# Layer 0 of a two-layer macaron model: query-state products on GpSimd, a fourth output chunk sorted by expert, and scratch rows cleared by nine writes

## The chip, the cores and the metric

The kernel runs on one core of a Trainium2 chip. The metric is the device time of one execution in microseconds (us), lower is better. The core has five engines with a queue of instructions each: TensorE (PE), VectorE (DVE), ScalarE (ACT), GpSimd (POOL) and SyncE (SP). Each engine takes its queue strictly in order, so an instruction that waits holds up everything behind it. DMA transfers are started from the queues of SP, ACT and POOL. A difference of about 0.5% (4.6 us) is what a measurement of this kernel can tell from no change.

## The reference

There are 8 sequences of 256 tokens with 128 features. Two layers follow each other, and each is feed-forward, attention, feed-forward, all with residuals. In layer 0 the feed-forward part sends each token to its two best of 8 experts (hidden width 512), and the attention is a delta-rule recurrence over time, for 16 heads of width 8:

```
def step(M, inp):
    q_t, k_t, v_t, b_t = inp
    out_t = einsum('bnh,bnhd->bnd', q_t, M)          # the query-state product
    retrieved = einsum('bnhd,bnd->bnh', M, k_t)
    delta = v_t - retrieved
    M = M + b_t[..., None, None] * einsum('bnh,bnd->bnhd', k_t, delta)
    return M, out_t
```

Step t needs the state that step t-1 left, so the 256 steps can't run side by side. Batch and head together (8 x 16) fill the 128 partitions. Layer 1 has ReLU attention, and experts (hidden width 256) that each choose their 256 best tokens.

## The kernel before

**Tiles and chunks.** A tile is 16 time steps of all 8 sequences, 128 tokens; there are 16 tiles (0 to 15). `CHUNKS` (line 30) groups them as 3, 4, 4, 3 and 2 tiles. Layer 0 is a pipeline over these chunks. "In" calls are the first feed-forward part (in 0, in 1 and in 2, where in 2 covers the last three chunks together). Then `prepare` (line 850) makes keys, values and queries of a chunk, `steps` (line 982) runs its part of the recurrence, `finish` (line 1050) turns states into attention output, and "out" calls (out 0 to out 4, one for each chunk) are the second feed-forward part.

**The recurrence** is on DVE: six small instructions a step (lines 1024 to 1038 and 1007), 16 steps a tile. When a tile's states are complete, `finish` multiplies them with the queries: one DVE instruction of 128 x 1024 a tile, `qm` (line 1064), with the normalised queries `qn` made once a chunk (line 972). PE adds up the products (`pm`, line 1070), ACT copies them, and two DMAs, a square, a mean, a root and a matmul follow until `x` is updated (line 1112).

**An expert call** comes in two forms. A *dense* call (`dense`, line 617) sends the chunk's tokens through all 8 experts: 32 matmuls of 128 x (128 n) for n tiles (line 639) and 32 n of 128 x 128 (line 649). A *sorted* call (`gates` 321, `route` 420, `scattering` 494, `fetching` 678, `experts` 697, `combining` 784) computes the two experts of each token, writes the tokens to DRAM rows ordered by expert with indirect DMAs on POOL's queue (line 503, two for each tile), reads them back (line 689), and runs one expert for each row tile: four 128 x 128 matmuls in (line 764) and four out (line 743). The results go to DRAM (line 727) and come back by indirect DMAs on POOL's queue (line 834), and matmuls add them up (lines 809 and 812). Each row tile loads its own expert's weights of 514 KB (line 568). Before, in 1, in 2, out 0, out 1 and out 2 are sorted; in 0, out 3 and out 4 are dense (line 226). The unfilled DRAM rows must be zero: `clearing` (line 519) writes 37 blocks of 128 x 256 numbers from the tile `zero`.

**The order of the work** is fixed when the program is built. A planner, `Weave` (line 42), runs generators; each yields an engine and an estimated time, and the planner gives the next place to the one that could start first, and among equals to the one of higher rank. The estimates only set the order on each queue: at run time semaphores decide. A yield on "pool" also charges DVE 0.5 us in the plan (line 100). Streams wait for marks such as ("states", t), ("x", key) or ("free", tag, number); `acquire` (line 600) hands out buffers. The gates of out c wait for `finish(c)` and for the result of out c-2 (line 1122), and PE takes the calls in the order in 0 to out 4 (line 1125). Layer 1 starts when PE is through with out 4 (line 1421) and when `moving` (line 1143) has carried the tokens into layer 1's layout: half 0 after chunk 2, half 1 after out 4 (line 1163).

Of the kernel before, what the change touches and what calls it, by code (L numbers as in the profile page):

```python
# [17 lines left out]
P = 128  # L18
# [9 lines left out]
F0, F1 = 512, 256  # L28

CHUNKS = [(0, 3), (3, 4), (7, 4), (11, 3), (14, 2)]  # L30
BANKS = {"h": 3, "y": 2, "m": 2, "f": 1}
CAP = B * S // E

SORTED = NT // 2
# [7 lines left out]
class Weave:  # L42
# [27 lines left out]
    def run(self, streams):  # L70
        for rank, s in streams:
            self.spawn(s, rank)
        streams, at, nexts = self.streams, self.at, self.nexts
        while any(n is not None for n in nexts):
            best = None
            for i, n in enumerate(nexts):
                if n is None:
                    continue
                if n[0] in self.free:
                    start = max(at[i], self.free[n[0]])  # L80
                elif n[0] == "until":
                    start = max(at[i], n[1])
                elif n in self.done:
                    start = max(at[i], self.done[n])
                else:
                    continue
                if best is None or (start, -self.ranks[i], at[i]) < best[:3]:
                    best = start, -self.ranks[i], at[i], i
            if best is None:
                raise RuntimeError([(st.__name__, n) for st, n in zip(streams, nexts) if n])  # L90
            start, _, _, i = best
            self.rank = self.ranks[i]
            if nexts[i][0] in self.free:
                engine, us, lag, table = nexts[i] + (None, None, LAGS[nexts[i][0]], None)[len(nexts[i]) :]
                if table and table != self.table:
                    self.load(table)  # L96
                    self.table = table
                    us += 1.3
                self.free[engine] = start + us
                if engine == "pool":  # L100
                    self.free["dve"] += 0.5
                start += us + lag
            at[i] = self.now = start
            nexts[i] = next(streams[i], None)
# [3 lines left out]
def kernel(ctx: ExitStack, tc: tile.TileContext, a: dict, out: bass.AP):  # L108
# [58 lines left out]

    x1 = const.tile([P, NT, D], F32, name="x1")

    zero = const.tile([P, 2 * D], F32, name="zero")  # L170
    pool.memset(zero, 0.0)
    rows0 = load("rows0", 5 * D + NH + 1, act)
    wqT, wkT, wvT, woT, b2 = (rows0[:, i * D : (i + 1) * D] for i in range(5))
    b2 = b2[:E, :]
# [21 lines left out]
    def woven(dram, moe, pools):  # L196
# [26 lines left out]
        calls["in", 2] = t0, NT - t0  # L223
        for c in range(n_c):
            calls["out", c] = CHUNKS[c]
        is_sorted = set(calls) - {("in", 0), ("out", n_c - 2), ("out", n_c - 1)}
        unsorted = [key for key in calls if key not in is_sorted]
        chosen = {}

# [10 lines left out]
        def vec(n):  # L240

            return "dve", 0.07 + 0.00105 * n, 0.14
# [145 lines left out]
        def turned_gates(key, g, m):  # L388

            name = "b" + "".join(map(str, key))  # L390
            gate = chosen[key]["gate"]
            if True:
                b = yield from acquire("m")
                yield "pe", 0.15 * m
                pg = bank("m", b, [E, TB, P], f"pg{name}_{g}")
                for i in range(m):
                    pe.transpose(pg[:, i, :], gate[:, g + i, :], ident)
                yield "act", 0.1 + 0.13 * m
                gT = work.tile([E, BW], F32, name=f"gT{name}_{g}", tag="gT", bufs=1)
                act.copy(gT[:, : m * P], pg[:, :m].rearrange("p a b -> p (a b)"))  # L400
                mark(("free", "m", b))
            return gT

        def biasing(key):

            t0, m = calls[key]
            gT = yield from turned_gates(key, 0, m)
            b = yield from acquire("m")
            yield "pe", 0.23 * m
            pb = bank("m", b, [P, TB, D], f"pb{key[0]}{key[1]}")  # L410
            for i in range(m):
                pe.matmul(pb[:, i, :], lhsT=gT[:, i * P : (i + 1) * P], rhs=b2, start=True, stop=True)
            xs = x[:, t0 : t0 + m, :]
            yield vec(m * D)
            dve.tensor_tensor(xs, xs, pb[:, :m], ALU.add)
            mark(("free", "m", b))
            mark(("biased", key))
# [91 lines left out]

        def dram_rows(i, nt):  # L510

            wide = -(-nt // 2) * 2
            rows = [
                nc.dram_tensor(f"rows_{i}_{k}", [m * P, D], F32, kind="Internal").ap()
                for k, m in enumerate((wide, nt))
            ]
            return rows

        def clearing():

            for k, ((rows, _), us) in enumerate(zip(buffers, (15.0, 45.0, 300.0, 340.0))):
                yield "until", us
                n = rows.shape[0] // P // 2
                for i in range(n):
                    yield "sp", 0.4, 2.0
                    sync.dma_start(
                        out=rows.rearrange("(r p w) d -> r p (w d)", p=P, w=2)[i], in_=zero
                    )
                mark(("clear", k))

# [253 lines left out]
        def combining(key, parts):  # L784


            t0, n = calls[key]
            name = "c" + "".join(map(str, key))
            yield "computed", key
            c = chosen[key]  # L790
            got = {}

            def joined(what, g, m):
                gT = yield from turned_gates(key, g, m)
                if m > 2:
                    yield "got", key, 2 * (g + m) - 5
                b = yield from acquire("m")
                pb = bank("m", b, [P, TB, D], f"pb{name}_{g}")
                for i in range(m):

                    gates = moe.tile([P, 2, P], F32, name=f"dg{name}_{g}_{i}", tag="dg")
                    for k in range(2):
                        yield "act", 0.28
                        act.activation(
                            gates[:, k, :], half_ident, AF.Copy, scale=c["p"][k][:, g + i : g + i + 1]
                        )
                    yield "got", key, 2 * (g + i) + 1
                    yield "pe", 0.75
                    pe.matmul(pb[:, i, :], lhsT=gT[:, i * P : (i + 1) * P], rhs=b2, start=True, stop=False)
                    for k in range(2):  # L810
                        j = 2 * (g + i) + k
                        pe.matmul(
                            pb[:, i, :], lhsT=gates[:, k, :], rhs=got.pop(j), start=False,
                            stop=k == 1,
                        )
                        mark(("back", key, j))
                xs = x[:, t0 + g : t0 + g + m, :]
# [149 lines left out]
        def queries(c, q, inverse):  # L967
            n = CHUNKS[c][1]
            inv = yield from inverse(2, q)
            qn = scan.tile([P, CT, HD], F32, name=f"qns{c}", tag="qn")[:, : n * SL]  # L970
            yield vec(2 * n * P)
            dve.tensor_tensor(qn, q.rearrange("p h t -> p t h"), bc(inv, HD), ALU.mult)
            prepared[c, "q"] = qn
            mark(("queries", c))

# [74 lines left out]
        def finish(c):  # L1050
# [5 lines left out]
            yield "queries", c  # L1056
            for i in range(n):
                yield "states", t0 + i
                yield "dve", 1.15
                qn = prepared[c, "q"]  # L1060
                M = states.pop(t0 + i)
                ts = slice(i * SL, (i + 1) * SL)
                qm = scan.tile([P, SL, HD, HD], F32, name=f"qm{name}_{i}", tag="qm")
                dve.tensor_tensor(qm, M[:, :, :, :HD], bc(qn[:, ts], HD), ALU.mult)  # L1064
                mark(("summed", t0 + i))
                yield "pe", 1.8

# [763 lines left out]
```

## Time and profile before

| what | value |
|---|---|
| median of 3 runs (lowest to highest) | 921.16 us (921.13 to 925.2) |
| the profiled execution: time, span of its profile | 919.45 us, 917.7 us |
| mean granted clock of PE | 0.884 |
| PE busy | 728.3 us, 79% |
| DVE busy | 537.8 us, 59% |
| ACT busy | 453.9 us, 49% |
| POOL busy | 153.9 us, 17% |
| tile 0 of the recurrence starts, tile 15 ends | 121.1 us, 453.9 us |
| PE on out 2 (sorted), out 3 (dense), out 4 (dense) | 435.6 to 475.2, 475.2 to 528.1, 528.1 to 557.7 us |

The profile gives, for one execution, the busy time of each engine, a picture of the span in 40 slices with a digit for the busy tenths of each slice, the chain of work that ended last, groups of equal instructions with their count, mean duration and the idle time in front of them, and tables of any stretch of time. All times in us count from the start of the span. A line Lnnn is the line of the kernel that issued the instruction.

### The profile page before, as it was taken

What the parts mean: (1) busy time and instruction counts of PE and PEld (TensorE: products, weight loads), DVE (VectorE), ACT (ScalarE), POOL (GpSimd) and SP (SyncE); (2) the same over time, 40 slices, a digit from 0 to 9 for tenths busy, and PEclk for the clock granted to TensorE, in tenths of its full rate; (3) what the DMA queues carried; (4) which work ended last, traced back from release to release, by engine and by line L of the source; (5) the groups of instructions that cost most, each with busy time, mean ns of one, the idle gap of its engine ahead of it and who ended that gap; (6) DMA issues with size and microseconds to landing.
All of it is one profiled execution on the core that took longest, in us unless ns stands there. A gap on an engine that the chain in (4) does not pass through costs nothing.

```text
span 917.7 us, 16688 instructions
## 1 busy us (share of the span) xinstructions
PE 728.3 (79%) x5243; PEld 586.6 (64%) x5243; DVE 537.8 (59%) x3223; ACT 453.9 (49%) x1067; POOL 153.9 (17%) x263
## 2 busy tenths in 40 slices
PE   3999559985399647854999999994889999999671
PEld 2778459884268437843997796763755556666471
DVE  2433176676599899887711422577347766658741
ACT  3556245772178604841674555431456666673231
POOL 0030712005400230033003000003031111100303
PEclk9999779997589657975899999898799999999976
DMA  4367585963557336926583331005210000000352
GB/s 187 104 176 207 151 261 180 268 211 101 187 143 234 80 127 196 244 63 200 160 252 96 113 113 30 0 1 162 89 55 2 2 2 2 2 1 0 119 157 76
DMA packets 101160, 109.07 MB, mean 119 GB/s; under 512 B 38736, under 2 KB 79056, under 8 KB 101072
## 3 DMA queue, kind: packets, MB, share of 16 engines
q1 hardware_dynamic: 96544, 98.42, 35.6%
q0 software_dynamic: 4096, 8.40, 2.9%
q10 hardware_dynamic: 432, 1.20, 0.4%
q8 instruction: 41, 0.67, 0.3%
q14 instruction: 47, 0.39, 0.1%
HBM read 85.11 MB, written 22.87 MB: 118 GB/s over the span
## 4 chain that ended last, share of the span: by engine, by line
PE 36%; DVE 15%; DMA 5%; ACT 4%; issue 4%; SPq 2%; POOL 1%; another core or an unknown queue 0%; POOLq 0%; DVEq 0%; ACTq 0%
PE ps L1636 3%; PE pa L1680 3%; PE phf L1436 3%; PE pydout L649 3%; PE phdout L639 3%; PE pyf L1453 3%; PE phpout L764 2%; DVE x L1483 2%; DVE ge0f L1321 2%; PE pypout L743 2%; PE pypf L743 2%; PE phpf L764 1%; PE pmo L1070 1%; DMA xs<-rows 1%; DVE ge1f L1321 1%
## 5 line engine op out<-in xcount | busy, mean ns | idle before, releaser
L1453 PEld LDWEIGHTS pyf<-w_W,hf 128*128 128x128 f32 x512 | 71.0, 200 | 26.0 <-issue 22.6
L1453 PE MATMUL pyf<-w_W,hf 128*128 128x128 f32 x512 | 76.0, 287 | 2.6 <-DVE x L1483 2.1
L1007 DVE TENSOR_TENSOR mk<-Ms,kns 128x72 f32<-128x72 f32 x251 | 56.3, 224 | 25.4 <-ACT Ms L961 23.7
L1436 PE MATMUL phf<-xTf,w_W 128*128 128x512 f32 x128 | 67.9, 616 | 0.0
L1442 ACT ACTIVATE hf<-phf 128x512 f32<-128x512 f32 x64 | 37.8, 597 | 59.9 <-PE phf L1436 57.6
L1070 PE MATMUL pmo<-qmo,ident 128*128 128x128 f32 x256 | 38.9, 314 | 29.3 <-DVE qmo L1064 19.4
L1034 DVE TENSOR_TENSOR Ms<-Ms,u 128x64 f32<-128x64 f32 x251 | 53.9, 215 | 13.6 <-DVE e L1002 8.3
L768 ACT ACTIVATE hpin<-phpin,w 128x128 f32<-128x128 f32 x160 | 45.7, 379 | 24.7 <-remote 12.3
L743 PE MATMUL pypin<-w,hpin 128*128 128x128 f32 x320 | 46.7, 295 | 13.3 <-ACT hpin L768 8.1
L768 ACT ACTIVATE hpout<-phpout,w 128x128 f32<-128x128 f32 x172 | 49.1, 374 | 16.4 <-PE phpout L764 14.8
L1002 DVE TENSOR_REDUCE e<-mk 128x8 f32<-128x72 f32 x251 | 54.6, 218 | 3.7 <-DVE u L1029 3.3
L1070 PEld LDWEIGHTS pmo<-qmo,ident 128*128 128x128 f32 x256 | 36.3, 226 | 32.0 <-DVE qmo L1064 21.8
L96 ACT ACT_TABLE_LOAD x43 | 55.2, 1283 | 3.0 <-issue 2.2
L1038 DVE SCALAR_TENSOR_TENSOR r<-kbs,dot,e 128x8 f32<-128x8 f32 x251 | 54.9, 219 | 2.8 <-DVE Ms L1034 2.7
L1029 DVE TENSOR_TENSOR u<-kbs,r 128x64 f32<-128x64 f32 x256 | 56.3, 220 | 0.2
L743 PEld LDWEIGHTS pypin<-w,hpin 128*128 128x128 f32 x320 | 43.3, 209 | 14.7 <-ACT hpin L768 8.9
L1652 DVE TENSOR_SCALAR w<-ps 128x512 f32<-128x512 f32 x64 | 42.5, 684 | 16.0 <-PE ps L1636 12.7
L764 PE MATMUL phpout<-xTpout,w 128*128 128x128 f32 x344 | 49.1, 290 | 2.2 <-ACT xTpout L718 2.2
L643 ACT ACTIVATE hdout<-phdout,w 128x384 f32<-128x384 f32 (+1 forms) x64 | 32.3, 526 | 34.0 <-PE phdout L639 26.9
L764 PE MATMUL phpin<-xTpin,w 128*128 128x128 f32 x320 | 47.5, 298 | 0.7 <-issue 0.7
L503 POOL DMA_INDIRECT rows<-xnf,slotrf x16 | 15.8, 985 | 188.7 <-DVE pastrf L479 184.3
L764 PEld LDWEIGHTS phpout<-xTpout,w 128*128 128x128 f32 x344 | 44.9, 205 | 3.4 <-ACT xTpout L718 3.2
(360 smaller groups left out, 1762.1 us busy)
## 6 DMA issues: line engine op xcount, KB each, us to landing
w<-in_w_dram SPq DMA_DIRECT2D x107, 514.0 KB
w<-in_w_dram SPq DMA_DIRECT2D x30, 256.0 KB
xs<-rows SPq DMA_DIRECT2D x24, 256.0 KB
rows<-zero SPq DMA_DIRECT2D x37, 128.0 KB
rows<-ypin SPq DMA_DIRECT2D x9, 256.0 KB
rows<-ypout SPq DMA_DIRECT2D x9, 256.0 KB
w_W<-in_w_dram SPq DMA_DIRECT2D x8, 256.0 KB
dts<-sps SPq DMA_DIRECT2D x6, 256.0 KB
```

The costliest lines, as they stand in the source:

```text
L96: self.load(table)
L743: pe.matmul(py[:, t % TB, :], lhsT=h[:, g, :], rhs=second(w, g), start=g == 0, stop=g == n_f - 1)
L764: pe.matmul(ph[:, f, :], lhsT=first(w, f), rhs=xT[:, t % TB, :], start=True, stop=True)
L768: act.activation(h[:, f, :], ph[:, f, :], AF.Relu, bias=bias(w, f))
L1002: dve.tensor_reduce(e, mk, AX.X, ALU.add)
L1007: dve.tensor_tensor(mk, M(t), bc_mid(kn[:, t + 1], HD), ALU.mult)
L1029: dve.tensor_tensor(u, bc(kb[:, t], HD), bc_mid(r, HD), ALU.mult)
L1034: dve.tensor_tensor(M(t + 1)[:, :, :HD], M(t)[:, :, :HD], u, ALU.add)
L1038: dve.scalar_tensor_tensor(r, kb[:, t], dot, e, ALU.mult, ALU.add)
L1070: pe.matmul(pm, lhsT=ident, rhs=qm[:, :, h, :], start=h == 0, stop=h == HD - 1)
L1436: pe.matmul(ph, lhsT=W[:, e, f * P : (f + 1) * P], rhs=c["xT"][k], start=True, stop=True)
L1453: pe.matmul(py[:, i, :], lhsT=before[0][ff][:, i * P : (i + 1) * P], rhs=second(W[:, before[3]], ff), start=ff == 0, stop=ff == n_f - 1,)
```

## The change

1. The products `qm` (16 of 128 x 1024) and the normalised queries `qn` (5) are issued on GpSimd in place of VectorE. The planner is told 2.4 us for a product and 0.2 + 0.3 n for queries of n tiles, and charges DVE 0.5 us only for GpSimd work under 1.5 us.
2. out 3 becomes a sorted call: 13 row tiles, in place of 8 experts on 3 tiles.
3. The 37 clearing writes become 9, of up to 12 tiles each, from the tile `x1`, which GpSimd sets to zero at the start and which nothing else uses until layer 1. The rows are no longer rounded up to even numbers of tiles.
4. The buffer `gT` of the turned gates gets a lock in the planner (`gates`, one place), freed after the matmuls that read it, and in `joined` the wait for gathered rows comes ahead of the turning of the gates.

```
-BANKS = {"h": 3, "y": 2, "m": 2, "f": 1}
+BANKS = {"h": 3, "y": 2, "m": 2, "f": 1, "gates": 1}
...
-                if engine == "pool":
+                if engine == "pool" and us < 1.5:
                     self.free["dve"] += 0.5
...
-    zero = const.tile([P, 2 * D], F32, name="zero")
-    pool.memset(zero, 0.0)
+    pool.memset(x1[:, : (NT + E) // 2, :], 0.0)
...
-        is_sorted = set(calls) - {("in", 0), ("out", n_c - 2), ("out", n_c - 1)}
+        is_sorted = set(calls) - {("in", 0), ("out", n_c - 1)}
...
-            if True:
-                b = yield from acquire("m")
...
-            return gT
+            room = yield from acquire("gates")
+            b = yield from acquire("m")
...
+            return gT, room
...
-                n = rows.shape[0] // P // 2
-                for i in range(n):
+                n = rows.shape[0] // P
+                for r in range(0, n, (NT + E) // 2):
+                    m = min(n - r, (NT + E) // 2)
                     yield "sp", 0.4, 2.0
                     sync.dma_start(
-                        out=rows.rearrange("(r p w) d -> r p (w d)", p=P, w=2)[i], in_=zero
+                        out=rows[r * P : (r + m) * P].rearrange("(p w) d -> p w d", p=P), in_=x1[:, :m, :]
                     )
...
             def joined(what, g, m):
-                gT = yield from turned_gates(key, g, m)
                 if m > 2:
                     yield "got", key, 2 * (g + m) - 5
+                gT, room = yield from turned_gates(key, g, m)
...
-            yield vec(2 * n * P)
-            dve.tensor_tensor(qn, q.rearrange("p h t -> p t h"), bc(inv, HD), ALU.mult)
+            yield "pool", 0.2 + 0.3 * n
+            pool.tensor_tensor(qn, q.rearrange("p h t -> p t h"), bc(inv, HD), ALU.mult)
...
-                yield "dve", 1.15
+                yield "pool", 2.4
...
-                dve.tensor_tensor(qm, M[:, :, :, :HD], bc(qn[:, ts], HD), ALU.mult)
+                pool.tensor_tensor(qm, M[:, :, :, :HD], bc(qn[:, ts], HD), ALU.mult)
```

Built, the change also alters the queues. On POOL, around the end of the recurrence, the order is now: the gathers of out 1, six of the eight scatters of out 2, the product of tile 14, the last two scatters of out 2, the product of tile 15, the six scatters of out 3. On PE, the sums of tile 14's products and the gates of out 3 come ahead of the experts of out 2, the combine of out 2 stands among the row tiles of out 3, the gates of out 4 behind the last of them, and the combine of out 3 among the dense experts of out 4. On DVE, the first step of chunk 1 now comes behind the update of `x` by `finish(0)`.

More of the change, by code (lines that the diff above doesn't have):

```diff
@@ L391, in turned_gates @@
             gate = chosen[key]["gate"]
-            if True:
-                b = yield from acquire("m")
[L394 to L401, printed above, removed]
-            return gT
+            room = yield from acquire("gates")
+            b = yield from acquire("m")
+            yield "pe", 0.15 * m
+            pg = bank("m", b, [E, TB, P], f"pg{name}_{g}")
+            for i in range(m):
+                pe.transpose(pg[:, i, :], gate[:, g + i, :], ident)
+            yield "act", 0.1 + 0.13 * m
+            gT = work.tile([E, BW], F32, name=f"gT{name}_{g}", tag="gT", bufs=1)
+            act.copy(gT[:, : m * P], pg[:, :m].rearrange("p a b -> p (a b)"))
+            mark(("free", "m", b))
+            return gT, room
         def biasing(key):
             t0, m = calls[key]
-            gT = yield from turned_gates(key, 0, m)
+            gT, room = yield from turned_gates(key, 0, m)
             b = yield from acquire("m")
@@ L412, in biasing @@
                 pe.matmul(pb[:, i, :], lhsT=gT[:, i * P : (i + 1) * P], rhs=b2, start=True, stop=True)
+            mark(("free", "gates", room))
             xs = x[:, t0 : t0 + m, :]
@@ L510, in dram_rows @@
         def dram_rows(i, nt):
-            wide = -(-nt // 2) * 2
             rows = [
-                nc.dram_tensor(f"rows_{i}_{k}", [m * P, D], F32, kind="Internal").ap()
-                for k, m in enumerate((wide, nt))
+                nc.dram_tensor(f"rows_{i}_{k}", [nt * P, D], F32, kind="Internal").ap() for k in range(2)
             ]
@@ L816, in joined @@
                         mark(("back", key, j))
+                mark(("free", "gates", room))
                 xs = x[:, t0 + g : t0 + g + m, :]
```

## The prediction

> **What bounds the kernel now.** I read the picture of the span first: which engine is full where.
>
> ```profile
> PE   3999559985399647854999999994889999999671
> DVE  2433176676599899887711422577347766658741
> POOL 0030712005400230033003000003031111100303
> PEclk9999779997589657975899999898799999999976
> ```
>
> A digit is 22.9 us. In slices 11 to 19 (252 to 459 us) DVE, which runs the recurrence, is at 8 or 9 tenths nearly throughout, and PE falls to 3 twice. From slice 20 to 27 (459 to 642 us) PE is full and DVE falls to 1 to 5. So two bounds follow each other: the recurrence on DVE until 454 us, then PE with out 2, out 3 and out 4. The table of stretches gives the prices: tile 4 (210.7), tile 11 (357.9), out 3 (475.2) and out 4 (528.1).
>
> ```profile
> core 0: us, PE busy (x) PEld busy (x) DVE busy (x) ACT busy (x) POOL busy (x), PEclk, DMA share, GB/s
> 210.70:240.20 29.50, 12.57 (x63) 9.56 (x63) 15.55 (x127) 4.58 (x13) 19.99 (x21) 0.60 0.53 176
> 357.90:369.70 11.80, 11.80 (x108) 11.80 (x107) 11.80 (x109) 7.50 (x25) 0.00 (x0) 1.00 0.84 268
> 475.20:528.10 52.90, 50.41 (x309) 39.97 (x308) 13.56 (x63) 26.53 (x52) 9.06 (x50) 1.00 0.40 124
> 528.10:557.70 29.60, 29.60 (x207) 27.67 (x206) 7.68 (x30) 15.80 (x35) 0.00 (x0) 1.00 0.26 82
> ```
>
> Sixteen bare steps take 11.8 us (tile 11). Tile 4, beside 21 indirect DMAs on POOL, takes 29.5. The chain of waits shows how the two bounds meet: out 2's rows arrive, PE goes through out 2, out 3 and out 4 without a break worth naming, and the second half of layer 1's input is loaded right behind.
>
> ```profile
> 429.38 6.14 DMA xs<-rows
> 435.57 1.13 PE ptpout L714 x4
> ...
> 473.37 1.79 PE pypout L743 x16
> 475.16 3.87 PE phdout L639 x12
> ...
> 555.04 2.69 PE pydout L649 x24
> 561.56 1.53 DMA xd<-x
> 563.31 3.98 DMA x<-xd
> ```
>
> From here every us by which out 4 ends earlier or later is carried to the end: layer 1 keeps its order on PE. So I sum the shift of out 4's end, 557.7.
>
> **Products on GpSimd: the price.** The groups by form:
>
> ```profile
> L1064 DVE TENSOR_TENSOR qmo<-Ms,qns 128x1024 f32<-128x1024 f32 x16 | 19.4, 1214 | 0.0
> L1589 POOL TENSOR_TENSOR xba<-xna,w_rows 128x256 f32<-128x256 f32 x8 | 5.9, 732 | 59.3 <-ACT xna L266 59.3
> ```
>
> On DVE a product delays the next step by 1.14 (the 1.21 of the row overlaps it a little). On POOL a quarter of it takes 0.73; with 0.09 fixed (a one-column memset on POOL takes 89 ns) the whole takes 0.64 x 4 + 0.09 = 2.65 us. `qn` of four tiles: 1.03 on DVE, 0.64 x 2 + 0.09 = 1.37 on POOL.
>
> What a product on POOL costs the recurrence beside it, the trace doesn't show: no GpSimd tensor_tensor runs there, and in layer 1 none lies beside a DVE instruction with two inputs in SBUF. I bound it.
> - At best nothing: DVE gains 1.14 for each tile.
> - The middle row is tile 4. Of its 17.7 us over the bare time, 3.3 are other DVE work and 3.05 one wait for PE; the other 11.3 over 21 indirect DMAs make 0.54 for each 0.95 us of POOL, 57%. For 2.65 that is 1.5, a net loss of 0.4 a tile.
> - At worst DVE stands still for all of the 2.65: a net loss of 1.5. A row shows such a standstill: two equal instructions on DVE, the second beside a memset on POOL.
>
> ```profile
> 472.31 0.23 DVE L1185 TENSOR_SCALAR row_e<-row_e 128x128 int32<-128x128 int32 x1
> 472.49 0.50 DVE L1186 TENSOR_SCALAR row_e<-row_e 128x128 int32<-128x128 int32 x1
> ```
> ```profile
> 472.50 0.42 POOL L1561 MEMSET va<- 128x334 f32 x1
> ```
>
> The second took 0.50 for 0.23 and ended 0.07 behind the memset's end (472.92): it waited the memset out whole. Five of the six instructions of a step read two SBUF tensors, as a product on POOL also does, and this is the row nearest to compute work on both engines. I take the worst end as the likeliest, and keep all three.
>
> [...]
>
> **Shift of the recurrence at the end of tile 14** (435.6 now), the point that matters below. Products of tiles 3 to 13 lie in front of it, 11 of them; those of tiles 0 to 2 only meet DVE's wait for chunk 1 (172.7 to 192.3). Four `qn` lie there too (0.6 to 1.0 on DVE, 0.86 on average; 0.3 dearer on POOL). The first step of chunk 1 now stands behind `finish(0)`, whose update of `x` came at 193.5, behind the start at 190.2: +3. Against that, DVE stood idle for others (PE, ACT, DMA) in waits over 0.3 us for about 15 us between 200 and 436, of which I let half absorb a loss, or half as much (3) eat a gain.
> - Worst: 11 x 1.5 + 1.2 + 3 - 7 = +14.
> - Middle: 11 x 0.4 + 1 + 3 - 2 = +6.
> - Best: -11 x 1.14 - 3.4 + 3 + 3 = -10.
>
> **A wait that the change adds on POOL.** Behind the product of tile 14 stand out 2's last two scatters. Now the scatters run free of it:
>
> ```profile
> 416.40 1.04 POOL L503 DMA_INDIRECT rows<-xngout,slotrout  x1 [7.82 <-issue]
> ...
> 425.36 0.98 POOL L503 DMA_INDIRECT rows<-xngout,slotrout  x1 [0.30 <-issue]
> ```
>
> The last ends at 426.3, and PE gets the rows 9.2 later (landing, SP's read, transposes at 435.57). Behind the product they end at 435.7 + 2.65 + 0.3 + 2.25 = 440.9, and PE starts at 450.1: **+14.6**, plus the shift of tile 14. Who waits: SP's read of the rows, then PE, which has nothing else placed ahead. The gathers of out 1, now behind the product of tile 13 (411.7), come some 16 us later than 398.6; they delay out 3's gates, not yet the path.
>
> **PE on out 2** took 39.6. The sums of tile 14 (2.3), the gate matmuls of out 3 (1.2) and the bias of dense out 3 (1.4) leave this stretch, out 3's routing matmuls (2) come in: **-2.6**.
>
> **out 3 sorted, and out 4.** A row tile is eight 128 x 128 matmuls, 0.89 for four (rows L764 and L743, two records a matmul): 1.78. Thirteen: 23.1; transposes 2; out 2's combine in between 3.5; filling the pipeline 2: 30.6. Then out 4's gates: from the update of `x` by out 2 to the router matmuls 6.8 passed, of which 2.4 lie beside the last row tile: 4.4. Dense out 4: 29.6 as now, plus out 3's combine 2.8, plus gates, bias and heads that stood in out 3 (2.6), plus 3 for gathers that PE meets early: the first combine of out 2 came 13.4 behind its last expert, PE now asks after 11. That is 38. In all 73, against 82.5 now (475.2 to 557.7): **-9.5**. The saving on matmuls alone is larger: dense out 3 is 32 x 0.645 + 96 x 0.2225 = 42, sorted 23.1. The rest is spent on the way to DRAM and back. Five more weight loads of 514 KB hide: 13 in 30 us is 226 GB/s, and tile 11's stretch moved 268. If they don't, each costs 1.9. out 3's scatters come behind the product of tile 15: 454 + 14 + 2.65 + 0.3 + 7.6 + 9.2 = 488, and out 2's experts hold PE until 501, so they are covered.
>
> **Clearing and locks** I cost at nothing. The nine writes fall between 5 and 62 us and near 300 and 340; PE has one idle stretch over 1 us between its first matmul at 13.35 and 100 us, and weights are held five ahead. If a write of 786 KB at 200 GB/s stood in front of a needed load it would cost 4. The larger memset takes POOL about 1 us more at 2.2 us; its next DMA is at 46.6. The lock orders matmuls that PE has to do anyway.
>
> **Sum.** Worst end: 14.6 + 14 - 2.6 - 9.5 = +16.5. Middle: +8.5. Best: -7.5. The profiled execution took 919.45 (span 917.7), the median of the runs 921.16, 1.7 more, so I state medians: 937.7, 929.7 and 913.7.
>
> **The rivals.**
> - *DVE is stopped by POOL* (forecast): 938. For it: the memset row. Against it: single DVE instructions beside indirect DMAs are hardly longer.
> - *DVE is freed* (the other side): the products run beside the recurrence, 1.14 a tile is gained, tile 14 ends near 426 instead of 450, and the rows of out 2 wait only for the product. 914, and down to 903 where the queues, laid out for a fast recurrence, meet fewer waits (+14.6 shrinks by 11, as the two scatters come ready with the product). It decides as soon as a product costs DVE under 0.6 us: 11 x (0.6 - 1.14) with the waits and `qn` puts tile 14 under -2.5, and the sum under 0. Against it: five of six instructions share inputs with POOL.
> - *Half a stop*, the middle row: 930.
> - *It doesn't do what it says*: the built queues hold 21 tensor_tensor on POOL and 13 row tiles for out 3, so I leave that out.
>
> **Chances.** Stopped 0.52, half 0.13, freed 0.35. By a spread of 8 us about each, faster by over 0.5% (below 916.5) 0.37, within 0.5% (about what a measurement of this kernel can tell from no change) 0.07, slower 0.56. The range takes in all three: 902 to 952; the upper end lets waits absorb nothing (+7) and the strided `qn` take double. The likeliest case alone: 928 to 952.
>
> **What would show it.** In the profile after, 16 steps beside a product: one gap of about 2.5 us in DVE for each tile (right), none (freed). Tile 14 ends near 450. PE starts out 2 near 464, out 3 near 501, out 4 ends near 574, and the stretch from out 3 to the end of out 4 is 73 long. A product that takes POOL 4 us or more, or a gather queue that holds products up by tens of us, would make me wrong on both ends.

## The result, and the profile after

The changed kernel takes 933.36 us (median of 9 runs, 927.7 to 935.8), the kernel before 921.58 in the same session (9 runs). The ratio is 1.011, with a 95% interval of 1.008 to 1.014: slower by more than this kernel's measurement leaves open. The forecast was 938. Here and below, ratios leave out executions more than 1.5% above the fastest of the same kernel, and the columns from profiles leave out the one profile of such an execution (that of route_early), so a ratio is not always the quotient of two medians. The profiled execution took 934.17, with a span of 932.3: 14.6 longer than the span before.

The picture of the span, changed kernel:

```profile
PE   4999649976596628937887899995888999999672
DVE  2433279295799999959200322577436767648741
POOL 1021461016422250162213010003031121100303
PEclk9999779995798658975898979799798999999866
```

A digit is 23.3 us here. DVE leaves its plateau with slice 19 (443 us), where before kept it until slice 20 (459 us), so the loss is not in the recurrence. It is in PE's row behind it: slices 19 to 22 (443 to 536 us) hold 8 8 7 8 where before had 9 9 9 9, and the clock in slices 21 to 25 is 8 9 7 9 7 where it was 9 9 9 9 8.

The table of stretches, for tile 4, tile 11, out 2, out 3 and out 4 of the changed kernel:

```profile
core 0: us, PE busy (x) PEld busy (x) DVE busy (x) ACT busy (x) POOL busy (x), PEclk, DMA share, GB/s
210.30:238.50 28.20, 15.41 (x63) 12.27 (x63) 16.20 (x128) 5.86 (x14) 17.36 (x18) 0.50 0.51 175
350.50:364.10 13.60, 13.60 (x101) 13.49 (x102) 13.60 (x109) 7.96 (x25) 2.03 (x1) 0.85 0.58 169
440.80:486.20 45.40, 40.09 (x295) 38.68 (x295) 8.80 (x36) 25.22 (x75) 11.48 (x85) 0.86 0.67 208
486.20:525.80 39.60, 33.60 (x251) 31.57 (x251) 1.76 (x7) 21.68 (x72) 7.63 (x8) 0.91 0.70 211
525.80:569.50 43.70, 41.90 (x246) 36.62 (x246) 12.81 (x63) 21.70 (x48) 5.68 (x6) 0.88 0.31 94
```

Tile 11, sixteen bare steps and one product on POOL, takes 13.6 for 11.8. Out 2 and out 3 have 5.3 and 6.0 us without PE, and all three stretches a clock of 0.86 to 0.91, where out 3 and out 4 had 1.00.

What a product does to DVE is best seen beside tile 11's product. POOL first, then DVE:

```profile
362.00 2.03 POOL L1065 TENSOR_TENSOR qmo<-Ms,qns 128x1024 f32<-128x1024 f32 x1 [12.76 <-DVE r L1039]
```
```profile
361.33 0.23 DVE L1030 TENSOR_TENSOR u<-kbs,r 128x64 f32<-128x64 f32 x1
...
362.10 2.01 DVE L1030 TENSOR_TENSOR u<-kbs,r 128x64 f32<-128x64 f32 x1
364.03 0.21 DVE L1003 TENSOR_REDUCE e<-mk 128x8 f32<-128x72 f32 x1
```

The same instruction, `u`, took 0.23 in the step before and 2.01 beside the product, and ended 0.08 behind it. DVE stood still, but the profile shows no gap: the wait lies inside one instruction. Whoever looks for idle time misses it.

Where the 14.6 us lie, from marks that both profiles have:

| mark | before | after | shift |
|---|---|---|---|
| tile 14 of the recurrence ends | 435.6 | 425.4 | -10.2 |
| first expert matmul of out 2 (L764) | 437.4 | 440.8 | +3.4 |
| out 4 ends (L649) | 557.7 | 569.5 | +11.8 |
| end of the span | 917.7 | 932.3 | +14.6 |

So the recurrence gave 10, the way from it to out 2 took 13.6, out 2 to out 4 took 8.4, and layer 1 took 2.8.

Between the end of tile 14 and out 2, SP and PE of the changed kernel did this:

```profile
432.18 3.61 SPq L1156 DMA_DIRECT2D xd<-x  x8
436.11 4.42 SPq L689 DMA_DIRECT2D xs<-rows  x4
```
```profile
428.17 3.62 PE L1071 MATMUL pmo<-qmo,ident 128*128 128x128 f32 x16
435.56 1.24 PE L341 MATMUL ptgout<-ident,xngout 128*128 128x128 f32 x3 [3.78 <-ACT xngout L266]
437.38 1.45 PE L354 MATMUL plgout<-w_few,xTgout 128*128 128x8 f32 x6 [0.57 <-ACT xTgout L344]
439.03 1.11 PE L714 MATMUL ptpout<-ident,xs 128*128 128x128 f32 x4 [0.20 <-DMA xs<-rows]
```

The last scatter of out 2 ended at 429.8. The rows' load (L689) was issued at 436.1, behind eight stores of out 1's `x` (L1156), which started at 432.2, when out 1's late combine had updated `x`. On PE the sums of tile 14 and the router of out 3 stood in front as well.

Inside out 3 the largest gap of PE is this one. POOL runs the eight gathers of out 2; ACT and PE stop:

```profile
492.18 0.99 POOL L835 DMA_INDIRECT ygcout<-rows,slotrout  x1 [20.85 <-DMA rows<-ypout]
...
501.00 0.95 POOL L835 DMA_INDIRECT ygcout<-rows,slotrout  x1 [0.30 <-issue]
```
```profile
497.65 0.63 ACT L768 ACTIVATE hpout<-phpout,w 128x128 f32<-128x128 f32 x2
503.54 0.57 ACT L400 COPY gTbout<-pgbout 8x512 f32<-8x512 f32 x1 [5.27 <-remote]
```
```profile
498.36 1.06 PE L743 MATMUL pypout<-w,hpout 128*128 128x128 f32 x8
...
500.69 0.49 PE L764 MATMUL phpout<-xTpout,w 128*128 128x128 f32 x3 [0.72 <-issue]
505.20 2.08 PE L743 MATMUL pypout<-w,hpout 128*128 128x128 f32 x8 [4.02 <-ACT hpout L768]
```

ACT did nothing for 5.27 us although the matmuls that it waits for were done by 497.2 ("remote": the profile knows no releaser on this core). PE waited 4.02 for it, and then four matmuls (eight records, x8) took 2.08 where they took 1.06: the granted clock had fallen by half.

### The profile page after: what moved, and what is told of

The parts are those of the page before. It is cut to its first block, busy times and chain, and to the rows that moved or that the text cites. A ratio compares the mean times of both kernels' runs of the same rounds, so it can differ in the third digit from the quotient of the medians.

```text
span 932.3 us, 16768 instructions
## 1 busy us (share of the span) xinstructions
PE 731.6 (78%) x5236; PEld 597.0 (64%) x5236; DVE 540.4 (58%) x3186; ACT 457.0 (49%) x1102; POOL 203.7 (22%) x296
## 5 line engine op out<-in xcount | busy, mean ns | idle before, releaser
L768 ACT ACTIVATE hpout<-phpout,w 128x128 f32<-128x128 f32 x224 | 63.8, 374 | 34.8 <-PE phpout L764 23.9
L743 PE MATMUL pypout<-w,hpout 128*128 128x128 f32 x448 | 64.0, 291 | 7.3 <-ACT hpout L768 7.3
L764 PE MATMUL phpout<-xTpout,w 128*128 128x128 f32 x448 | 65.0, 294 | 3.9 <-DMA w<-in_w_dram 1.8
L1035 DVE TENSOR_TENSOR Ms<-Ms,u 128x64 f32<-128x64 f32 x251 | 61.9, 246 | 8.8 <-DVE e L1003 5.0
L1030 DVE TENSOR_TENSOR u<-kbs,r 128x64 f32<-128x64 f32 x256 | 64.3, 251 | 0.1
L743 PEld LDWEIGHTS pypout<-w,hpout 128*128 128x128 f32 x448 | 59.1, 206 | 8.0 <-ACT hpout L768 7.9
L764 PEld LDWEIGHTS phpout<-xTpout,w 128*128 128x128 f32 x448 | 60.3, 209 | 5.0 <-DMA w<-in_w_dram 2.2
L768 ACT ACTIVATE hpin<-phpin,w 128x128 f32<-128x128 f32 x160 | 45.9, 381 | 25.7 <-remote 8.7
L1065 POOL TENSOR_TENSOR qmo<-Ms,qns 128x1024 f32<-128x1024 f32 x16 | 32.0, 2001 | 119.8 <-DVE r L1039 98.5
L1653 DVE TENSOR_SCALAR w<-ps 128x512 f32<-128x512 f32 x64 | 42.5, 684 | 18.2 <-PE ps L1637 14.2
L1071 PE MATMUL pmo<-qmo,ident 128*128 128x128 f32 x256 | 43.2, 340 | 8.5 <-DVE x L1113 7.0
L764 PE MATMUL phpin<-xTpin,w 128*128 128x128 f32 x320 | 46.0, 291 | 4.4 <-DMA w<-in_w_dram 3.7
L1025 DVE CUSTOM_DVE_ANT_0 rk<-r,kns 128x8 f32<-128x8 f32 x251 | 47.2, 188 | 3.7 <-DVE mk L1008 3.4
```

The source lines that it names most:

```text
L743: pe.matmul(py[:, t % TB, :], lhsT=h[:, g, :], rhs=second(w, g), start=g == 0, stop=g == n_f - 1)
L764: pe.matmul(ph[:, f, :], lhsT=first(w, f), rhs=xT[:, t % TB, :], start=True, stop=True)
L768: act.activation(h[:, f, :], ph[:, f, :], AF.Relu, bias=bias(w, f))
L1030: dve.tensor_tensor(u, bc(kb[:, t], HD), bc_mid(r, HD), ALU.mult)
L1035: dve.tensor_tensor(M(t + 1)[:, :, :HD], M(t)[:, :, :HD], u, ALU.add)
L1653: dve.tensor_scalar(w, ps, 0.0, None, ALU.max)
```

## The experiments

Twelve kernels were run in three sessions on three chips. Before took 876.4, 926.9 and 922.0 us on them; ratios are to before in the same session. The changed kernel was run on the second of these chips alone (after_again), and before was profiled only for the first result, so positions in us are compared within a chip where that is possible and else with that in mind. "Stretch" is from out 2's first expert matmul to out 4's end, "idle" is PE's in it, "clock" PE's granted clock over it.

| run | median | ratio [95%] | tile 14 ends | out 2 starts | stretch | idle | clock |
|---|---|---|---|---|---|---|---|
| before, first profile | 921.6 | 1 | 435.6 | 437.4 | 120.4 | 2.9 | 0.98 |
| changed, first profile | 933.4 | 1.011 [1.008, 1.014] | 425.4 | 440.8 | 128.7 | 13.1 | 0.88 |
| clear_only | 878.8 | 1.001 [0.998, 1.004] | 398.9 | 402.1 | 117.0 | 0.4 | 0.99 |
| prod_only | 883.2 | 1.009 [1.007, 1.011] | 398.9 | 404.9 | 116.7 | 2.8 | 0.99 |
| sort_only | 884.0 | 1.006 [1.004, 1.009] | 408.9 | 409.9 | 117.5 | 6.3 | 0.93 |
| no_prod | 888.0 | 1.010 [1.007, 1.014] | 400.5 | 413.4 | 117.5 | 9.2 | 0.93 |
| after_again | 935.4 | 1.010 [1.007, 1.014] | 432.9 | 448.2 | 129.2 | 11.4 | 0.86 |
| prod_twice | 953.9 | 1.031 [1.025, 1.036] | 449.3 | 464.5 | 128.4 | 12.5 | 0.89 |
| scat_first | 934.7 | 1.011 [1.006, 1.016] | 438.1 | 451.7 | 125.3 | 9.8 | 0.89 |
| route_early | 940.6 | 1.014 [1.009, 1.019] | - | - | - | - | - |
| both_late | 931.3 | 1.015 [1.007, 1.022] | 435.4 | 445.0 | 126.0 | 13.2 | 0.92 |
| gather_plain | 919.8 | 1.002 [0.998, 1.005] | 429.0 | 444.5 | 116.5 | 9.3 | 0.93 |
| no_sort | 920.1 | 1.001 [0.997, 1.005] | 427.9 | 443.0 | 113.2 | 0.0 | 0.99 |
| all_three | 929.9 | 1.012 [1.003, 1.020] | 435.6 | 445.2 | 122.9 | 9.3 | 0.90 |

### The parts, one at a time

**prod_only**, part 1 alone, on the kernel before:

```
-                if engine == "pool":
+                if engine == "pool" and us < 1.5:
...
-            dve.tensor_tensor(qn, ...)
+            pool.tensor_tensor(qn, ...)
...
-                dve.tensor_tensor(qm, ...)
+                pool.tensor_tensor(qm, ...)
```

> Before with part 1 alone: the state products and the normalised queries on GpSimd, nothing else changed. Theory A (the products free DVE, and what is lost is lost behind tile 14): the recurrence's tile 14 ends near 425 instead of 435.6, PE starts out 2 near 441 instead of 435.6 because two scatters stand behind the product of tile 14, and the time is 4 to 8 us above before (926 to 930). Theory B (GpSimd stops DVE for the whole product; the early end in the changed kernel comes from the clearing or from the sorting): tile 14 ends at 440 or later, PE starts out 2 at 455 or later, and the time is 938 or more.

Measured: 1.009. Tile 14 ends at 398.9, exactly where it ends in clear_only, which has the DVE work of before and ran on the same chip: neither 10 earlier nor later (tile 3 starts 4.0 later, at 177.2, and the way from there is 4.1 shorter). Out 2 starts 2.8 later. So both theories missed on the recurrence: on this chip the products neither free nor delay it. From tile 3's start to tile 14's end DVE is busy for 209.1 us instead of 199.4, and idle for 12.6 instead of 26.3: the stops are paid out of waits. The profiled execution, the quickest of the four, is no longer than clear_only's (span 877.0 and 877.3), so where the 0.9% of the timed runs lies is not shown.

**no_prod**, the changed kernel with part 1 undone:

```
-            pool.tensor_tensor(qn, ...)
+            dve.tensor_tensor(qn, ...)
...
-                pool.tensor_tensor(qm, ...)
+                dve.tensor_tensor(qm, ...)
```

> The changed kernel with part 1 undone: products and normalised queries back on DVE, out 3 still sorted, still nine clearing writes. Theory A: tile 14 ends near 435 as before, PE starts out 2 near 436, and out 3 and out 4 still take about 83 us together, as long as the dense out 3 did, because the added scatters and gathers stop ACT and PE; the time is 922 to 930. Theory B: tile 14 keeps its early end near 425 without the products on GpSimd, and PE starts out 2 near 426; the time is 910 to 918.

Measured: 1.010; tile 14 ends at 400.5, close to clear_only's 398.9, so the early end is not kept from the other parts. Out 2 starts 12.9 behind the end of tile 14, where Theory A had 1: a long delay although no product stands among the scatters. Slower without any product on GpSimd: sorting out 3 alone costs.

**clear_only**, part 3 alone:

```
-    zero = const.tile([P, 2 * D], F32, name="zero")
-    pool.memset(zero, 0.0)
+    pool.memset(x1[:, : (NT + E) // 2, :], 0.0)
...
-                for i in range(n):
+                for r in range(0, n, (NT + E) // 2):
```

> Before with part 3 alone: the scratch rows cleared by nine large writes in place of 37 small ones. Theory A: no difference, 919 to 924, tile 0 starts at 121 and tile 14 ends near 435. Theory B: the large writes give the recurrence its early start (114) and tile 14 ends 7 to 10 us earlier; the time is 911 to 916.

Measured: 1.001, and the interval takes in 1. The clearing is free and gives nothing. Tile 0 starts at 101.0 on this chip with small writes (102.0 in prod_only) or large ones.

**sort_only**, parts 2 and 4 alone:

```
-        is_sorted = set(calls) - {("in", 0), ("out", n_c - 2), ("out", n_c - 1)}
+        is_sorted = set(calls) - {("in", 0), ("out", n_c - 1)}
```

> Before with parts 2 and 4 alone: out 3 sorted by expert, with the lock on the gates; products on DVE, small clearing writes. By the forecast's own sum (out 3 and out 4 in 73 us, out 2 2.6 shorter or longer) the time is 912. Theory A (the six scatters and six gathers that out 3 adds stop ACT and through it PE, and TensorE's granted clock falls behind each stop): out 3 and out 4 take 80 to 84 us, out 2 two to six us more than 39.6, and the time is 921 to 928. Theory B: 908 to 914.

Measured: 1.006. The stretch is 117.5 against clear_only's 117.0: sorting saves nothing. Theory A's place holds, its cause only in part: on this chip PE has no gap at all beside the gathers of out 2. What it has is 1.4 us of waiting for out 3's rows, 1.9 for out 4's router, 1.0 for out 3's gathers, and a clock of 0.93 instead of 0.99.

### The changed kernel again, and three edits of it

**after_again**, no edit.

> The changed kernel itself, unchanged, on the same chip as the runs to compare it with. If its parts add up (products +0.9%, sorting +0.6%, clearing 0), its ratio to before is 1.013 to 1.017; if the two parts share one loss (the same wait in front of out 2), 1.008 to 1.011.

Measured: 1.010, as in the first session, on another chip. Tile 14 ends 7.5 us later than in the first profile while the span grows by only 1.2: a single profile places the end of the recurrence no better than that.

**prod_twice**:

```
                 pool.tensor_tensor(qm, M[:, :, :, :HD], bc(qn[:, ts], HD), ALU.mult)
+                pool.tensor_tensor(qm, M[:, :, :, :HD], bc(qn[:, ts], HD), ALU.mult)
```

> The changed kernel with every state product issued twice in a row on GpSimd, into the same tile: the output stays, one more 2.0-us product a tile. Theory 1 (a product stops DVE for as long as it runs: beside it one DVE instruction of 0.2 us takes 1.9 and ends 0.1 behind it): tile 11 grows from 13.6 to 15.6, the recurrence up to tile 14 ends 11 x 2.0 = 22 us later less what DVE's idle time absorbs (7 to 13), so 9 to 15 later than in the unchanged kernel, and the time is 11 to 19 us above it. Theory 2 (the long instruction is an effect of the record, DVE is free): tile 11 stays 13.6, tile 14 ends where it did, and the time is 2 to 4 us above, from the scatters behind the second product.

Measured: 18.5 us above after_again, tile 14 16.4 later, DVE busy 224.1 instead of 203.5 between tile 3 and tile 14. Tile 11 has POOL's two products and two long instructions on DVE, the dot product `rk` of L1025 (1.93 us from 381.08) and the sum into the state:

```profile
381.02 1.97 POOL L1065 TENSOR_TENSOR qmo<-Ms,qns 128x1024 f32<-128x1024 f32 x1 [12.71 <-DVE r L1039]
383.07 1.97 POOL L1066 TENSOR_TENSOR qmo<-Ms,qns 128x1024 f32<-128x1024 f32 x1
```
```profile
383.26 1.86 DVE L1035 TENSOR_TENSOR Ms<-Ms,u 128x64 f32<-128x64 f32 x1
```

Theory 1 holds: DVE's 20.6 us more are 1.87 for each of the 11 products added there, which is nearly the 1.97 that one runs, and a further 2 us a tile go to the end of tile 14 for the most part (16.4 of 22). Behind it nothing more is lost: the stretch is 128.4 (129.2 in after_again). Tile 11 itself stayed 13.6 from its first to its last `u`: the second stop fell behind its last step, so the sum over the tiles carries the reading, not this tile.

**scat_first**:

```
+                if t0 + i == NT - 2:
+                    yield "routed", ("out", 2)
                 yield "pool", 2.4
```

> The changed kernel with one wait more in the planner: the product of tile 14 is queued on GpSimd behind all of out 2's scatters instead of ahead of the last two. Theory 1 (those two scatters, which stood ready, set the start of out 2): PE starts out 2 about 10 us behind the scatters' end, before or with the end of tile 14 instead of 15 us behind it, and the time is 5 to 10 us below the unchanged kernel. Theory 2 (PE would then only wait for weights or stand longer between out 2 and out 3): out 2 starts earlier, out 4 ends within 3 us of where it did, and the time is the same.

Measured: no change (1.011). The scatters ended at 429.0, 9.1 ahead of tile 14's end, and out 2 started at 451.7, 13.6 behind it. The scatters behind the product were not what out 2 waited for. My first theory of that delay, the forecast's, falls here.

**route_early**:

```
-                return flat(shape, n, f"{tag}{name}", f"{tag}k", F32, 2)
+                return flat(shape, n, f"{tag}{name}", f"{tag}k", F32, 3)
...
-                        yield "x", ("out", key[1] - 2)
+                        yield ("routed", ("out", 3)) if key[1] == 4 else ("x", ("out", key[1] - 2))
```

> The changed kernel with the router of out 4 waiting for out 3's scatters instead of for out 2's update of x, with a third buffer for the gates: nothing in out 4's own rows depends on out 2. Theory 1 (what the sorting saved on matmuls went into PE's idle time between out 3 and out 4 and into the lower granted clock behind it): the gap in front of out 4 (3 us on this chip) goes, out 4's own stretch falls from 43 to 36 to 39, from out 2's start to out 4's end it takes 109 to 113 instead of 117, and the time is 4 to 8 us below the unchanged kernel. Theory 2 (the saving is lost to the gathers of out 3 and to ACT, not to this gap): out 2's start to out 4's end stays 116 or more and the time is within 2 us.

Measured: 1.014, no gain. Both theories took 117 for the unchanged stretch, the quicker chip's; here it is 129.2. In the one profile, of an execution of 950.5 us, PE goes from out 3 to out 4 without a gap (out 4's first matmul starts at 541.1), but a wait of 2.6 us for out 4's weights and one of 2.1 beside out 3's gathers stand behind it. As far as this profile tells, Theory 2 is nearer.

### What out 2 and the sorted stretch wait for

**both_late**, the edit of scat_first and this one:

```
             for c, (t0, n) in enumerate(CHUNKS):
+                if c == 1:
+                    yield "fetched", ("out", 2), 0
                 yield "x", ("out", c)
```

> The changed kernel with two queue orders changed: on GpSimd the product of tile 14 stands behind all of out 2's scatters, and on SP the eight stores of out 1's x stand behind the first loads of out 2's rows instead of ahead of them. Theory 1 (out 2's start is set by SP's stores, which wait for out 1's late combine; that is why the scatters alone gave nothing): PE starts out 2 6 to 9 us behind the end of tile 14 instead of 13 to 15, directly behind the sums of tile 14, and the time is 4 to 8 us below the changed kernel (ratio to before 1.002 to 1.006). Theory 2 (PE's own order, the sums of tile 14 and out 3's router ahead of out 2's rows, sets it): out 2 starts 13 us or more behind the end of tile 14, and the time is the changed kernel's (ratio 1.010).

SP and PE of this kernel:

```profile
430.40 1.48 SPq L689 DMA_DIRECT2D xs<-rows  x3
440.00 3.97 SPq L1160 DMA_DIRECT2D xd<-x  x8
```
```profile
436.88 2.98 PE L1073 MATMUL pmo<-qmo,ident 128*128 128x128 f32 x16
439.69 0.60 PE L714 MATMUL ptpout<-ident,xs 128*128 128x128 f32 x4
443.57 1.25 PE L341 MATMUL ptgout<-ident,xngout 128*128 128x128 f32 x3 [3.27 <-ACT xngout L266]
445.02 1.22 PE L764 MATMUL phpout<-xTpout,w 128*128 128x128 f32 x4 [0.21 <-ACT xTpout L718]
```

The rows are now loaded ahead of the stores, at 430.4 instead of 436.1, and PE turns them directly behind the sums of tile 14. But the next instruction in PE's order is out 3's router, which waits 3.27 us for ACT, and the experts stand behind it. Out 2 starts 9.6 behind tile 14 instead of 13.6 to 15.4. Part of each theory: SP's order held 4 to 6 us, PE's own order holds most of the rest. In the time nothing is gained that this run could show: the interval reaches from 1.007 to 1.022.

**gather_plain**:

```
-                yield "pool", 1.27, 0
+                plain = key in (("out", 2), ("out", 3))
+                yield ("sp", 0.4, 0) if plain else ("pool", 1.27, 0)
...
-                pool.indirect_dma_start(
+                if plain:
+                    sync.dma_start(out=y, in_=dram_of[key][1][j * P : (j + 1) * P])
+                else:
+                  pool.indirect_dma_start(
```

> The changed kernel with the gathers of out 2 and out 3 as plain DMAs from SP, of the same size, from consecutive rows: it leaves out that the rows are picked by slot, so the two updates of x add other rows than they should. Theory 1 (a run of back-to-back indirect DMAs on GpSimd stops ACT, and PE waits for ACT): the idle time of PE of 3 to 5 us beside out 2's eight gathers and the lower clock behind it go; from out 2's start to out 4's end it takes 4 to 8 us less than in the changed kernel (129 where before takes 122), and the ratio to before is 1.002 to 1.006. Theory 2 (ACT stops there for its own reason, or SP's queue with 14 more DMAs holds up the weights): that stretch stays within 2 us, and the ratio is 1.009 or more.

Out 2, out 3 and out 4 of this kernel:

```profile
444.50:488.00 43.50, 39.27 (x291) 38.11 (x292) 8.69 (x35) 24.11 (x73) 11.49 (x85) 0.86 0.66 211
488.00:521.00 33.00, 30.74 (x258) 29.05 (x257) 1.76 (x7) 22.97 (x74) 0.00 (x0) 1.00 0.73 228
521.00:561.00 40.00, 37.18 (x246) 33.48 (x246) 12.98 (x63) 21.83 (x49) 0.00 (x0) 0.96 0.40 129
```

Measured: 1.002 [0.998, 1.005] against 1.010, and a stretch of 116.5 against 129. Out 3 takes 33.0 instead of 39.6, at a clock of 1.00 instead of 0.91. In the whole stretch PE waits 6.1 us for weights, likely the price of 14 more DMAs on SP, and still the stretch is 12 shorter. ACT has no wait there that the profile can't put down to another engine; the changed kernel has three of 3.0 to 5.3 us. Theory 1 holds: it is the fourteen indirect gathers on GpSimd (eight of out 2, six of out 3) that cost the stretch these 12 us, less what the places that the edit also moved on PE and ACT may give. By which path they stop ACT is not shown.

**no_sort**, the changed kernel with out 3 dense:

```
-        is_sorted = set(calls) - {("in", 0), ("out", n_c - 1)}
+        is_sorted = set(calls) - {("in", 0), ("out", n_c - 2), ("out", n_c - 1)}
```

> The changed kernel with out 3 dense again; products on GpSimd, nine clearing writes and the lock stay. If sorting out 3 saves nothing (shown by the two earlier runs without products, 1.006 and 1.010), the ratio to before is that of the products alone, 1.006 to 1.010, so 0 to 4 us below the changed kernel, and from out 2's start to out 4's end it takes 117 to 123. By the forecast's sum (sorting out 3 gains 12 us from out 2's start to out 4's end) it would be 10 us or more above the changed kernel, a ratio of 1.02.

```profile
443.00:476.70 33.70, 33.70 (x284) 33.39 (x285) 8.01 (x30) 24.21 (x74) 5.67 (x79) 0.95 0.71 221
476.70:526.50 49.80, 49.80 (x310) 39.93 (x310) 13.65 (x63) 26.45 (x52) 7.71 (x8) 1.00 0.43 140
526.50:556.20 29.70, 29.70 (x207) 27.77 (x207) 7.69 (x30) 15.81 (x35) 0.00 (x0) 1.00 0.25 79
```

Measured: 1.001 [0.997, 1.005]. The three rows show PE busy for every one of the 113.2 us. With out 3 sorted, the same kernel has 11 to 13 idle us and takes 129 on the two other chips where before takes 921 to 927. So on a chip of this speed the sorting is the whole loss, and products, clearing and the lock cost nothing that shows.

**all_three**, the edits of both_late and of route_early together.

> The changed kernel with the two queue orders of the run on out 2's start and with the early router of out 4 (its own run took the gap in front of out 4 away, from 3 us to 0, but a wait for weights of 2.6 us came in its place). If out 2's start is gained (4 to 8 us) and the early router gives 0 to 4 more, the ratio to before is 0.997 to 1.004: then this is the best form of the change, and no better than before. If the two gains are given back as waits for weights, it stays at 1.008 or more.

Measured: 1.012 [1.003, 1.020]. The stretch falls from 129 to 122.9, and out 2 starts 9.6 behind tile 14, but this is no better than before. None of the twelve kernels is faster than before.

## Why the prediction came out right, and where it was wrong

The time (933 for 938), the side and the range held. The working did not: two steps were wrong by 20 to 24 us, with opposite signs, so that the sum came within 2 us is luck. Measured against the execution that the sum was made for:

| step of the forecast | forecast | measured |
|---|---|---|
| tile 14 of the recurrence | +14 | -10.2 |
| from tile 14 to out 2 | +14.6 | +13.6 |
| out 2 to out 4, sorted | -12.1 | +8.4 |
| layer 1 | 0 | +2.8 |
| sum | +16.5 | +14.6 |

**The stop was right.** "I take the worst end as the likeliest": DVE stands still for the whole product. The pair of lines of tile 11 shows it, and prod_twice shows that it goes into the time. The forecast's own row for it was another case: a memset, which has no input, beside a DVE instruction with one. Here a two-input DVE instruction took 2.01 us beside a two-input product of 2.03; whether the number of inputs matters, as the forecast took it to, no run shows. "One gap of about 2.5 us in DVE" is wrong in form: it is one long instruction.

**Its price was too high.** "The whole takes 0.64 x 4 + 0.09 = 2.65 us" was scaled from a row a quarter of the size; 16 products took 32.0 us, 2.00 each. The net loss of a tile is 13.6 - 11.8 - 1.14 = 0.66, not 1.5. Over 11 products that is 7.3 instead of 16.5.

**The 7 us that waits were to absorb were too little.** The +3 for a later start of chunk 1 was 0.6 (tile 3 starts at 192.9, before at 192.3). Between tile 3's start and tile 14's end DVE is as busy as before (203.8 us, 203.0 before) and idle for 28.7 instead of 40.4; in three more executions with the same order up to there (after_again, gather_plain, no_sort) for 30.7 to 34.3. In these four, tile 14 ended at 425 to 433: 3 to 10 us earlier than in the one profile of before, instead of 14 later; in scat_first, both_late and all_three, with another order there, at 435 to 438, as in before. The 10 of the table is thus the best case of several, and prod_only against clear_only shows 0. Which waits went is not settled. I had read DVE at 8 or 9 tenths as a bound; one sixth of that time was idle, and that was enough to take up the stops.

**The delay of out 2 had its size, not its cause.** The forecast put +14.6 down to the two scatters behind the product. scat_first took the product out of their way, and out 2 still came 13.6 behind tile 14; no_prod has no product on GpSimd and 12.9. What held out 2 up stands in other queues: SP's stores of out 1's `x` ahead of the rows' load, and out 3's router ahead of out 2's experts on PE, which the forecast had with "nothing else placed ahead". Two of its sentences fail: the gathers of out 1 "come some 16 us later than 398.6; they delay out 3's gates, not yet the path". They came 1.7 later (400.3). Late was the combine that uses them. ACT turns to it with the copy `gTbout`, in before first, in the changed kernel behind a root of `finish(2)` (`rmo`). Before, then changed, ACT and SP:

```profile
399.02 0.56 ACT L400 COPY gTbout<-pgbout 8x512 f32<-8x512 f32 x1
420.51 2.26 SPq L1155 DMA_DIRECT2D xd<-x  x5
```
```profile
416.62 0.26 ACT L1099 ACTIVATE rmo<-pro,eps 128x3 f32<-128x3 f32 x1 [8.42 <-remote]
420.18 0.58 ACT L400 COPY gTbout<-pgbout 8x512 f32<-8x512 f32 x1 [3.30 <-remote]
```

The copy comes 21 us later, behind two waits of ACT, 8.42 and 3.30 us, while and just after POOL ran fourteen indirect DMAs without a break (400.3 to 417.8), although the matmuls that the first of them waits for were done at 408.9. So out 1's `x` was ready at 432.2 instead of 420.5, and SP's stores of it, which stand in front of the rows, started then. How much of this the order of the queue costs and how much the waits, no run takes apart.

**The sorting: the matmuls were right, what surrounds them was not.** Take from each stretch its idle time and, for the clock, its length times what the clock lacks of 1. Left are 115 in before and 112 in no_sort, and 100 in both profiles of the changed kernel and 99 in gather_plain: 12 to 16 us of bare work saved. The forecast's sum for the same stretch is 108, of which some 9 are waits (2 to fill the pipeline, 4.4 for out 4's gates, 3 for late gathers), so 99 of bare work: its matmuls were right. But the idle time is 13, not 9, and the lower clock takes 15 (128.7 x 0.12; it counts idle time in, so the split is rough), where the forecast had nothing for the clock and nothing for stops of ACT. The profile of before showed such a stop: ACT waited 4.6 us up to 493.4, beside the gathers of out 2, but PE, busy with the dense out 3, lost 1.5 by it. The forecast doesn't mention it.

**Clearing at nothing** held: 1.001 in clear_only, with an interval that takes in 1. The lock was not run alone; no_sort, which has it, shows no loss.

**Small slips.** In slices 11 to 19 of the picture PE falls to 4 twice, not to 3, and it is full up to slice 26, not 27. The four terms of PE on out 2 add up to -2.9, not -2.6. Nothing above rests on these.

**What stays open.** The products cost 0.9% on the chip where before takes 876 (prod_only) and nothing where it takes 922 (no_sort). Both intervals are narrow; the second kernel also has the clearing and the lock. No run tells which it is, the chip or the difference in the queues.

## What to carry to other kernels

A saving on one engine is worth what that engine's neighbours let it keep: before a dense stage is replaced by a sorted one, count the gathers and scatters that it adds and ask what PE does while they run; a dense stage that never waits was worth more here than 12 us of matmuls. Moving the products to GpSimd moved them out of DVE's queue but not out of DVE's time: look for single DVE instructions as long as the GpSimd one (here 2.01 us beside 2.03), not for gaps. And where a delay has the predicted size, take away its supposed cause once before believing it: here other queues held the work up just as long.

## What the runs showed of the hardware

In the changed kernel a 128 x 1024 product of two SBUF tensors took GpSimd 1.96 to 2.06 us; beside it one DVE instruction took 1.9 to 2.6 (0.2 alone) and ended 0.02 to 0.09 behind it, for 15 of the 16 products.

The chips differed in what ACT did beside a run of indirect DMAs. In the first session's before, tile 0 of the recurrence starts at 121.1 and ACT waits three times for 4.9 to 7.4 us beside 18 scatters from 90 to 113; in clear_only, on the quicker chip, tile 0 starts at 101.0. In front of `hpin`, the 160 ACT instructions of the in calls that two of these waits precede, ACT is idle for 13.0 us in all in clear_only, 12.1 of them for PE, and for 14.2 to 16.2 in the other three profiles of that chip; in before it is 24.7 and in the changed kernel 25.7, and the largest part there, 12.3 and 8.7, has no releaser on this core. The two spans differ by 40, and 35 of that lie in front of out 2 (437.4 and 402.1). What makes chips differ so is not settled.

In the changed kernel TensorE's granted clock fell behind a gap: after 4.02 us without work four matmuls (eight records) took 2.08 instead of 1.06, and the clock stayed at half (0.50) for 6.8 us (504.8 to 511.6). It did so for 6.8 us (463.8 to 470.6) behind a gap of 2.57 us too, and not behind one of 1.79 us (1.00 from 480.1 to 487.0). The clock also fell by half from 538.9 to 549.2, and no gap of PE in the 9 us ahead of that is longer than 0.3; that is not explained.
